# A fixed order for the projection steps of a perceiver layer, and low parts made one step earlier

## The chip, the core and the metric

The kernel runs on one core of a Trainium2 chip. The metric is the device time of one execution in microseconds. The core has five engines with a queue each, which run in order and wait for one another through semaphores: TensorE (PE, with its weight loads PEld), VectorE (DVE), ScalarE (ACT), GpSimd (POOL) and SyncE (SP), which issues nearly all DMAs here.

## What is computed

A perceiver layer over 128 latent rows of width 512. Its three blocks are a cross-attention of the normalised x over a context of 12544 rows, a chunked linear attention, and a quantised feed-forward part. Only the first block matters here:

```python
q = (inputs_q @ Wq).reshape(b, sq, H, HD) * (1.0 / np.sqrt(HD))
k = (inputs_kv @ Wk).reshape(b, skv, H, HD)
v = (inputs_kv @ Wv).reshape(b, skv, H, HD)
scores = jnp.einsum('bqhd,bkhd->bhqk', q, k)
attn = jax.nn.softmax(scores, axis=-1)
ctx = jnp.einsum('bhqk,bkhd->bqhd', attn, v).reshape(b, sq, H * HD)
return ctx @ Wo
```

with 16 heads of 128. The layer then goes on with `x = x + ...` for this block and the other two.

## The kernel before

**Projection stage.** q is projected and multiplied by Wk at once, so that the scores can be taken against the context itself. The loop over `h2` (eight pairs of heads) runs `project_q(h2 + 1)` ahead of `project_k(h2)`: PE makes `pq` (L205), ACT scales it into `qT` (L213), PE makes `pk` from `qT` and `wk` (L221), ACT copies `pk` into `b` in two halves (L230). In the text pq0 to pq7, qT0 to qT7, pk0 to pk7, b0 to b7 are these for each `h2`. Pairs 0 to 3 give the first half of the heads (f = 0), pairs 4 to 7 the second (f = 1); each half has two tiles `b` in a pool of three buffers.

**Strassen operands.** The products of the score stage are done in seven products instead of eight (Strassen-Winograd), each in three float32r products of high and low parts. `operands` makes the sums of the right side on DVE (L240: b11, t2, b12, b21), and `put` makes an operand's high part with an ACT cast (L233) and its low part with a DVE subtraction (L234). The names are B11, T2, T3, T1, T4, B21, B22. Half 0 is put during the projection loop, half 1 beside the first score units (the list `beside`). For the left side `sum_ct` makes four sums of a context block on DVE (L157 to L160) and `split_ct` its high part `cth` on ACT (L166) and its low part on DVE (L167).

**Score stage.** `scores` runs 49 blocks times 2 halves; a unit has 42 matmuls (L300). Its first product p1 needs A11 and B11, the second, p6, S2 and T2. p5 takes a second product only when DVE has read its first into c22 (L325). Results go to DRAM.

**Weighing stage.** 196 steps of 24 matmuls (L362): `soften(k)` subtracts the maximum on DVE (L410) and takes exp on ACT (L411), `high_part(k)` casts on ACT (L416) to `ph`, `low_part(k)` subtracts on DVE (L421) to `pl`, `total(k)` adds up on DVE (L429), `cut_hi` and `cut_lo` do the same split for the context rows (`ch` L398, `cl` L404). At a few steps `jobs` insert other work, among them an all-reduce of the sums on POOL (L554).

**Order.** A scheduler places instructions on the engines; those wrapped in `seq` keep their program order. Before, in the projection stage only the last sum of `sum_ct` is wrapped; in the weighing stage all steps are. `reuse` of a tile makes the next writer wait for the last reader. Weights are loaded into `ctp`'s tags "hi" and "lo", two buffers each, and pairs 2 and 3 into tiles of the right pool, `kq1p`. The DMA queue holds eight loads in flight.

Of the kernel before, what the change touches and what calls it, by code (L numbers as in the profile page):

```python
# [8 lines left out]
F32 = mybir.dt.float32  # L9
# [7 lines left out]
P = 128  # L17
# [3 lines left out]
HD = 128  # L21
# [12 lines left out]
def tile_perceiver_layer(  # L34
# [106 lines left out]
    def right(f, s, n):  # L141

        if (f, s) not in kq:
            kq[f, s] = (kq0p, kq1p)[f].tile([P, 2, 2, 512], F32R, name=f"kq{f}_{s}")
        return kq[f, s][:, n, :, :]

    def load_ct(i):
        if i == 1:
            raw = kq1p.tile([P, 8, 2, P], F32, name=f"kq1_{B22}")
        else:  # L150
            raw = ctp.tile([P, 8, 2, P], F32, tag="raw", name="ctr", bufs=1)
        nc.sync.dma_start(out=raw[:, A11:, :, :], in_=cT[i])
        return raw

    def sum_ct(raw):
        r = lambda s: raw[:, s, :, :]
        nc.vector.tensor_tensor(r(S1), r(A21), r(A22), ALU.add)  # L157
        nc.vector.tensor_tensor(r(S3), r(A11), r(A21), ALU.subtract)
        nc.vector.tensor_tensor(r(S2), r(S1), r(A11), ALU.subtract)
        seq(nc.vector.tensor_tensor(r(S4), r(A12), r(S2), ALU.subtract))  # L160

    def split_ct(raw, lo=None):
        hi = ctp.tile([P, 7, 2, P], F32R, tag="hi", name="cth")
        if lo is None:
            lo = ctp.tile([P, 7, 2, P], F32R, tag="lo", name="ctl")
        nc.scalar.copy(hi, raw[:, :7, :, :])  # L166
        nc.vector.tensor_tensor(lo, raw[:, :7, :, :], hi, ALU.subtract)  # L167
        return hi, lo


    with tc.tile_pool(name="ps_pro", bufs=2, space=PSUM) as ps_pro:

        def load_w(h2):

            hs = slice(h2 * 256, (h2 + 1) * 256)
            if h2 in (2, 3):
                both = kq1p.tile([P, 2, 1024], F32, name=f"kq1_{h2 + 2}")
                wq = both[:, 0, :].rearrange("p (c e) -> p c e", c=NC)
                wk = both[:, 1, :].rearrange("p (h d) -> p h d", h=2)
            else:  # L180
                wq = ctp.tile([P, NC, 256], F32, tag="hi", name="wq")
                wk = ctp.tile([P, 2, D], F32, tag="lo", name="wk")
            nc.sync.dma_start(out=wq, in_=x_wq[:, hs].rearrange("(c p) e -> p c e", p=P))
            nc.sync.dma_start(out=wk, in_=x_wkT[hs, :].rearrange("(h p) d -> p h d", p=P))
            return wq, wk

        keep_warm(ps_pro, 9)
        ws = [load_w(h2) for h2 in range(4)]
        raw = load_ct(0)
        xn = mxp.tile([P, D], F32, tag="mx1", name="xn")  # L190
        layernorm(xn, x0, D)

        warm = const.tile([P, 1], F32, name="warm")
        seq(nc.scalar.activation(warm, x0[:, 0:1], AF.Exp))
        xnT = tmp.tile([P, NC, P], F32, tag="u3", name="xnT")
        pt = ps_pro.tile([P, NC, P], F32, tag="q", name="pt")
        for i in range(NC):
            nc.tensor.transpose(pt[:, i, :], xn[:, i * P : (i + 1) * P], ident)
        nc.vector.tensor_copy(xnT, pt)

        def project_q(h2):
            pq = ps_pro.tile([P, 2, P], F32, tag="q", name="pq")
            for j in range(2):
                for cc in range(NC):
                    nc.tensor.matmul(  # L205
                        pq[:, j, :],
                        lhsT=ws[h2][0][:, cc, j * HD : (j + 1) * HD],
                        rhs=xnT[:, cc, :],
                        start=(cc == 0),
                        stop=(cc == NC - 1),  # L210
                    )
            qT = tmp.tile([P, 2, P], F32, tag=("p1", "u2")[h2 % 2], name="qT")
            nc.scalar.mul(qT, pq, HD**-0.5)  # L213
            return qT

        def project_k(h2, qT, b):

            pk = ps_pro.tile([P, 2, 2, 256], F32, tag="k", name="pk")
            for cc in range(NC):
                for j in range(2):  # L220
                    nc.tensor.matmul(  # L221
                        pk[:, cc // 2, cc % 2, j * P : (j + 1) * P],
                        lhsT=ws[h2][1][:, j, cc * P : (cc + 1) * P],
                        rhs=qT[:, j, :],
                        start=True,
                        stop=True,
                    )
            o = h2 % 2 * 256
            for a in range(2):
                nc.scalar.copy(b[h2 // 2 % 2][:, a, :, o : o + 256], pk[:, a, :, :])  # L230

        def put(f, s, v):
            nc.scalar.copy(right(f, s, 0), v)  # L233
            nc.vector.tensor_tensor(right(f, s, 1), v, right(f, s, 0), ALU.subtract)  # L234

        def operands(f, b):

            (b11, b21), (b12, b22) = ((t[:, 0, :, :], t[:, 1, :, :]) for t in b)
            t2 = mxp.tile([P, 2, 512], F32, tag=f"mx{f}", name="t2")
            sub = lambda out, x, y: nc.vector.tensor_tensor(out, x, y, ALU.subtract)  # L240
            return [
                lambda: sub(b11, b12, b11),
                lambda: sub(t2, b22, b11),
                lambda: put(f, T2, t2),
                lambda: sub(b12, b22, b12),
                lambda: put(f, T3, b12),
                lambda: put(f, T1, b11),
                lambda: sub(b21, b21, t2),
                lambda: put(f, T4, b21),
                lambda: put(f, B22, b22),  # L250
            ]

        qT = project_q(0)
        for h2 in range(8):
            if h2 + 4 < 8:
                ws.append(load_w(h2 + 4))
            if h2 == 1:
                raw1 = load_ct(1)
            nxt = project_q(h2 + 1) if h2 + 1 < 8 else None
            if h2 % 4 == 0:  # L260
                b = [iop.tile([P, 2, 2, 512], F32, tag="io", name="b") for _ in range(2)]
            project_k(h2, qT, b)
            qT = nxt
            if h2 == 1:
                put(0, B11, b[0][:, 0, :, :])
                put(0, B21, b[0][:, 1, :, :])
            if h2 == 2:
                sum_ct(raw)
            if h2 == 3:
                rest = operands(0, b)  # L270
                for do in rest[:6]:
                    do()
            if h2 == 5:
                cts = {0: split_ct(raw, mbp.tile([P, 7, 2, P], F32R, name="mb"))}
                for do in rest[6:]:
                    do()

    both = mbp.tile([P, 2, 1024], F32, name="mb")
    mb = [both[:, f, :] for f in range(2)]
# [2 lines left out]
    ps_s = psx.enter_context(tc.tile_pool(name="ps_s", bufs=8, space=PSUM, reuse_waits="tile"))  # L282
    beside = operands(1, b)
    beside[6:6] = [lambda: put(1, B21, b[0][:, 1, :, :])]
    beside[:0] = [
        lambda: (sum_ct(raw1), cts.update({1: split_ct(raw1)})), lambda: put(1, B11, b[0][:, 0, :, :]),
    ]

    def more():
        if beside:  # L290
# [61 lines left out]
    def weigh_operand(tag, n):  # L352
        return prp.tile([P, 1024], F32R, tag=tag, name=tag, bufs=n)
# [52 lines left out]
    def soften(k):  # L406
        f, i, j = step(k)
        if f is not None:
            exps[k] = scs[f, i][:, j, :]
            seq(nc.vector.tensor_tensor(exps[k], exps[k], mb[f], ALU.subtract))  # L410
            seq(nc.scalar.activation(exps[k], exps[k], AF.Exp))  # L411
# [5 lines left out]

    def low_part(k):
        if k < len(steps):
            low[k] = weigh_operand("pl", 2)  # L420
            seq(nc.vector.tensor_tensor(low[k], exps[k], high[k], ALU.subtract))  # L421

    def total(k):
        f, i, j = step(k)
        if f is not None:
            if i == 0 and j == 0:
                seq(nc.vector.tensor_copy(lsum[f], exps[k]))
            else:
                seq(nc.vector.tensor_tensor(lsum[f], lsum[f], exps[k], ALU.add))  # L429
# [5 lines left out]
    for i, f in units:  # L435
# [18 lines left out]
        while beside and (i, f) == (1, 0):  # L454
            more()
        if i + 1 not in cts and i + 1 < NP and i > 0 and (f == 1 or i == NP - 2):
            sum_ct(raw)
            cts[i + 1] = split_ct(raw)
        if (i, f) == (NP - 1, 0):
            nc.gpsimd.partition_all_reduce(mb[0], mx[0], P, bass_isa.ReduceOp.max)  # L460
    load_scores(2)
# [102 lines left out]
    at(4 * NP - 3, lambda: wo.update({1: by_rows(x_wo, 1, score_tile)}))  # L564

    with tc.tile_pool(name="ps_u", bufs=1, space=PSUM, reuse_waits="tile") as ps_u:
        total(0)
        soften(2)
        load_scores(4)
        for k, (f, i, j) in enumerate(steps):  # L570
            first, last = i == 0 and j == 0, i == NP - 1 and j == 1
# [13 lines left out]
                            seq(nc.scalar.copy(dst, old[b][cc]))  # L585
            high_part(k + 2)
            cut_hi(k + 2)
            low_part(k + 1)
            soften(k + 3)
            cut_lo(k + 1)  # L590
            total(k + 1)
            if k == 2:
                last_max()
            load_scores(k + 5)
            load_ctx(k + 3)
            weigh(pu, j, ctx_hi[f, i], ctx_lo[f, i], high.pop(k), low.pop(k), first, last)
            old = pu
            for job, args in jobs.pop(k, ()):
# [351 lines left out]
```

## Time and profile before

| | us |
|---|---|
| median of 3 runs | 2140.52 (2140.45 to 2141.22) |
| the profiled execution, its time | 2139.74 |
| its span | 2138.0 |
| projection stage, start to first score product | 0 to 37.3 |
| score stage | 37.3 to 972.7 |
| weighing stage | 972.7 to 2041 |
| rest of the layer | 2041 to 2138 |

The stages are read off the timeline of PE. In the table of groups a score or weighing matmul of 512 columns has a duration of 389 ns, but they are pipelined and follow each other every 0.227 us, so that a unit takes 9.52 us and a weighing step 5.44. In timeline lines the first two numbers are start and duration; in brackets stands how long the engine had been idle and which instruction ended that. In lists of waits the numbers are the total, how often, and the longest.

### The profile page before, as it was taken

The page shows a single profiled execution, that of the slowest core. Times are in us where ns is not written, and L with a number is a line of the kernel's source. Part 1 is how long each engine was busy: PE and PEld are TensorE (multiplying, and loading weights), DVE is VectorE, ACT ScalarE, POOL GpSimd, SP SyncE. Part 2 cuts the span into 40 slices and gives each one's busy share as a digit, 9 for nine tenths or more (in the row PEclk, how much of TensorE's full clock was granted, in tenths as well). Part 3 has the DMA queues.
Part 4 walks back from the last instruction along what each step waited for, and adds up shares of the span by engine and source line. Part 5 has one row for each costly group of instructions (what it writes and reads, how often), then busy time and mean ns, then how long its engine had stood idle before and what let it go on. Part 6 is the DMA issues. An engine that isn't in the chain of part 4 may idle for free.

```text
span 2138.0 us, 24043 instructions
## 1 busy us (share of the span) xinstructions
PE 2123.8 (99%) x9561; PEld 1739.7 (81%) x9566; DVE 1657.6 (78%) x1812; ACT 763.9 (36%) x843; POOL 24.8 (1%) x16
## 2 busy tenths in 40 slices
PE   9999999999999999999999999999999999999998
PEld 7888888888888888888888888888888888888874
DVE  6877777777777777778997888887887777777735
ACT  5222122221222212215444444444444444444423
POOL 0000000000000000000000000000100000000010
PEclk9999999999999999999999999999999999999999
DMA  6444444444444444446664455554444444444460
GB/s 221 149 172 160 169 177 157 167 162 163 177 160 165 167 158 177 165 150 226 222 231 151 170 173 186 187 187 148 138 148 148 141 140 144 147 148 148 139 205 9
DMA packets 77393, 350.36 MB, mean 164 GB/s; under 512 B 8000, under 2 KB 12352, under 8 KB 51808
## 3 DMA queue, kind: packets, MB, share of 16 engines
q1 hardware_dynamic: 77136, 348.69, 45.8%
q8 instruction: 75, 1.23, 0.2%
q14 instruction: 38, 0.31, 0.0%
q10 hardware_dynamic: 144, 0.13, 0.0%
HBM read 245.77 MB, written 103.02 MB: 163 GB/s over the span
## 4 chain that ended last, share of the span: by engine, by line
PE 96%; DVE 2%; issue 1%; DMA 0%; ACT 0%; DVEq 0%; SPq 0%
PE pu L362 49%; PE ps L300 43%; PE pc L629 1%; PE po L648 1%; DMA kq<-in_cT_dram 0%; PE pp L722 0%; DVE kq L234 0%; PE pq L205 0%; PE pw L92 0%; DVE b L240 0%; PE ph L848 0%; PE pp L782 0%; PE po L766 0%; PE psc L761 0%; PE pk L221 0%
## 5 line engine op out<-in xcount | busy, mean ns | idle before, releaser
L300 PE MATMUL ps<-kq,cth 128*128 128x512 f32 x2744 | 844.6, 389 | 0.0
L362 PE MATMUL pu<-ph,cl 128*128 128x512 f32 x1568 | 610.2, 389 | 1.4 <-DVE cl L404 1.2
L362 PE MATMUL pu<-pl,ch 128*128 128x512 f32 x1568 | 610.0, 389 | 0.0
L362 PE MATMUL pu<-ph,ch 128*128 128x512 f32 x1568 | 610.0, 389 | 0.0
L300 PEld LDWEIGHTS ps<-kq,cth 128*128 128x128 f32 x2744 | 515.0, 188 | 106.8
L300 PE MATMUL ps<-kq,ctl 128*128 128x512 f32 x1344 | 522.8, 389 | 0.0
L421 DVE TENSOR_TENSOR pl<-si,ph 128x1024 fp32r<-128x1024 f32 x194 | 241.3, 1244 | 203.5 <-PE pu L362 201.8
L362 PEld LDWEIGHTS pu<-ph,cl 128*128 128x128 f32 x1568 | 294.3, 188 | 63.2 <-DVE cl L404 2.2
L362 PEld LDWEIGHTS pu<-pl,ch 128*128 128x128 f32 x1568 | 294.3, 188 | 61.3
L362 PEld LDWEIGHTS pu<-ph,ch 128*128 128x128 f32 x1568 | 294.3, 188 | 61.1
L416 ACT CAST ph<-si 128x1024 fp32r<-128x1024 f32 x194 | 204.0, 1052 | 389.9 <-PE pu L362 389.8
L300 PEld LDWEIGHTS ps<-kq,ctl 128*128 128x128 f32 x1344 | 252.3, 188 | 52.5
L334 ACT COPY so<-ps 128x512 f32<-128x512 f32 x98 | 57.8, 589 | 577.0 <-PE ps L300 577.0
L411 ACT ACTIVATE si<-si 128x1024 f32<-128x1024 f32 x194 | 205.3, 1058 | 116.6 <-DVE si L410 116.4
L410 DVE TENSOR_TENSOR si<-si,mb 128x1024 f32<-128x1024 f32 x194 | 236.6, 1219 | 0.0
L429 DVE TENSOR_TENSOR lsum<-lsum,si 128x1024 f32<-128x1024 f32 x192 | 234.0, 1219 | 0.0
L343 DVE TENSOR_TENSOR mx<-mx,so 128x1024 f32<-128x1024 f32 x95 | 116.4, 1225 | 9.6
L338 DVE TENSOR_TENSOR so<-ps,u 128x512 f32<-128x512 f32 x98 | 67.7, 691 | 72.2 <-PE ps L300 72.2
L404 DVE TENSOR_TENSOR cl<-cr,ch 128x1024 fp32r<-128x1024 f32 x98 | 119.5, 1219 | 0.5 <-ACT ch L398 0.5
L332 DVE TENSOR_TENSOR mx<-mx,so 128x1024 f32<-128x1024 f32 x95 | 116.5, 1227 | 3.2
L398 ACT CAST ch<-cr 128x1024 fp32r<-128x1024 f32 x98 | 103.3, 1054 | 40.5 <-DMA cr<-in_c_dram 40.3
L328 DVE TENSOR_TENSOR so<-ps,u 128x512 f32<-128x512 f32 x98 | 67.7, 691 | 61.3 <-PE ps L300 61.3
(190 smaller groups left out, 1005.8 us busy)
## 6 DMA issues: line engine op xcount, KB each, us to landing
sc<-so SPq DMA_DIRECT2D x98, 1024.0 KB, 3.8
si<-sc SPq DMA_DIRECT2D x97, 1024.0 KB, 4.8
cr<-in_c_dram SPq DMA_DIRECT2D x98, 512.0 KB, 3.4
ctr<-in_cT_dram SPq DMA_DIRECT2D x94, 512.0 KB, 3.5
kq<-in_w1T_dram SPq DMA_DIRECT2D x16, 512.0 KB, 4.9
kq<-in_w2T_dram SPq DMA_DIRECT2D x16, 512.0 KB, 4.9
wq<-in_x_wq_dram SPq DMA_DIRECT2D x6, 512.0 KB, 5.2
wk<-in_x_wkT_dram SPq DMA_DIRECT2D x6, 512.0 KB, 6.1
```

The lines of the kernel that those rows point to most:

```text
L300: nc.tensor.matmul(ps, lhsT=lt[:, a, cc, :], rhs=right(f, b, part)[:, cc, :], start=(first and n == 0), stop=(n == 5), skip_group_check=True,)
L328: nc.vector.tensor_tensor(c21, p4, u3, ALU.add)
L332: nc.vector.tensor_tensor(mx[f], mx[f], so[:, 1, :], ALU.max)
L343: nc.vector.tensor_tensor(mx[f], so[:, 1, :] if i == 0 else mx[f], so[:, 0, :], ALU.max)
L362: nc.tensor.matmul(pu[b][cc], lhsT=lt[:, j, cs], rhs=rt[:, bs], start=(first and n == 0), stop=(last and n == 2))
L398: seq(nc.scalar.copy(ctx_hi[f, i], ctx_raw[f, i]))
L404: seq(nc.vector.tensor_tensor(ctx_lo[f, i], ctx_raw[f, i], ctx_hi[f, i], ALU.subtract))
L410: seq(nc.vector.tensor_tensor(exps[k], exps[k], mb[f], ALU.subtract))
L411: seq(nc.scalar.activation(exps[k], exps[k], AF.Exp))
L416: seq(nc.scalar.copy(high[k], exps[k]))
L421: seq(nc.vector.tensor_tensor(low[k], exps[k], high[k], ALU.subtract))
L429: seq(nc.vector.tensor_tensor(lsum[f], lsum[f], exps[k], ALU.add))
```

## The change

It does three things. In the projection stage, what `put`, `operands`, `sum_ct`, `split_ct`, `project_q` and `project_k` issue for half 0 and for context blocks 0 and 1 is wrapped in `seq`; the sums and splits get other places in the loop (block 0 at h2 = 2, T2 at 3, T3 and T1 at 4, T4 and B22 at 5, block 1 at 6 instead of beside the first score units). Weights of pairs 2 to 7 go into right-operand tiles of half 1 that are free until then, and all loads are issued ahead of the loop. `xnT` is copied in two halves by two engines. In the weighing stage `low_part` and `cut_lo` are made for step k + 2 instead of k + 1, `pl` gets a third buffer, and `load_ctx` goes from k + 3 to k + 4.

```diff
+    def spare(s, shape):
+        return kq1p.tile(shape, F32, name=f"kq1_{s}")
+    def in_turn(i, instruction):
+        return seq(instruction) if i < 2 else instruction
...
-    def sum_ct(raw):
+    def sum_ct(raw, i):
         r = lambda s: raw[:, s, :, :]
-        nc.vector.tensor_tensor(r(S1), r(A21), r(A22), ALU.add)
+        in_turn(i, nc.vector.tensor_tensor(r(S1), r(A21), r(A22), ALU.add))
...
-        nc.scalar.copy(hi, raw[:, :7, :, :])
-        nc.vector.tensor_tensor(lo, raw[:, :7, :, :], hi, ALU.subtract)
+        in_turn(i, nc.scalar.copy(hi, raw[:, :7, :, :]))
+        in_turn(i, nc.vector.tensor_tensor(lo, raw[:, :7, :, :], hi, ALU.subtract))
...
-            if h2 in (2, 3):
-                both = kq1p.tile([P, 2, 1024], F32, name=f"kq1_{h2 + 2}")
+            if h2 >= 2:
+                both = spare((B11, B21, T2, T3, T1, T4)[h2 - 2], [P, 2, 1024])
...
-        ws = [load_w(h2) for h2 in range(4)]
-        raw = load_ct(0)
+        ws, raws = [], {}
+        for what in (0, 1, 2, 3, "ct0", 4, 5, "ct1", 6, 7):
...
-        nc.vector.tensor_copy(xnT, pt)
+        nc.vector.tensor_copy(xnT[:, :2, :], pt[:, :2, :])
+        nc.scalar.copy(xnT[:, 2:, :], pt[:, 2:, :])
...
-            nc.scalar.mul(qT, pq, HD**-0.5)
+            seq(nc.scalar.mul(qT, pq, HD**-0.5))
...
-                nc.scalar.copy(b[h2 // 2 % 2][:, a, :, o : o + 256], pk[:, a, :, :])
+                seq(nc.scalar.copy(b[h2 // 2 % 2][:, a, :, o : o + 256], pk[:, a, :, :]))
...
-            nc.scalar.copy(right(f, s, 0), v)
-            nc.vector.tensor_tensor(right(f, s, 1), v, right(f, s, 0), ALU.subtract)
+            in_turn(2 * f, nc.scalar.copy(right(f, s, 0), v))
+            in_turn(2 * f, nc.vector.tensor_tensor(right(f, s, 1), v, right(f, s, 0), ALU.subtract))
...
             if h2 == 2:
-                sum_ct(raw)
+                sum_ct(raws[0], 0)
+                cts = {0: split_ct(raws[0], 0, mbp.tile([P, 7, 2, P], F32R, name="mb"))}
             if h2 == 3:
                 rest = operands(0, b)
-                for do in rest[:6]:
-                    do()
-            if h2 == 5:
-                cts = {0: split_ct(raw, mbp.tile([P, 7, 2, P], F32R, name="mb"))}
-                for do in rest[6:]:
-                    do()
+            for do in rest[slice(*{3: (0, 3), 4: (3, 6), 5: (6, 9)}.get(h2, (0, 0)))] if h2 >= 3 else ():
+                do()
+            if h2 == 6:
+                sum_ct(raws[1], 1)
+                cts[1] = split_ct(raws[1], 1)
...
-            low[k] = weigh_operand("pl", 2)
+            low[k] = weigh_operand("pl", 3)
...
+        low_part(1)
+        soften(2)
         total(0)
-        soften(2)
...
-            low_part(k + 1)
             soften(k + 3)
-            cut_lo(k + 1)
+            cut_lo(k + 2)
+            low_part(k + 2)
             total(k + 1)
...
-            load_ctx(k + 3)
+            load_ctx(k + 4)
```

More of the change, by code (lines that the diff above doesn't have):

```diff
@@ L145, in right @@
         return kq[f, s][:, n, :, :]
+    def spare(s, shape):
+        return kq1p.tile(shape, F32, name=f"kq1_{s}")
+    def in_turn(i, instruction):
+        return seq(instruction) if i < 2 else instruction
     def load_ct(i):
         if i == 1:
-            raw = kq1p.tile([P, 8, 2, P], F32, name=f"kq1_{B22}")
+            raw = spare(B22, [P, 8, 2, P])
         else:
@@ L153, in load_ct, with split_ct @@
         return raw
-    def sum_ct(raw):
+    def sum_ct(raw, i):
         r = lambda s: raw[:, s, :, :]
-        nc.vector.tensor_tensor(r(S1), r(A21), r(A22), ALU.add)
-        nc.vector.tensor_tensor(r(S3), r(A11), r(A21), ALU.subtract)
-        nc.vector.tensor_tensor(r(S2), r(S1), r(A11), ALU.subtract)
+        in_turn(i, nc.vector.tensor_tensor(r(S1), r(A21), r(A22), ALU.add))
+        in_turn(i, nc.vector.tensor_tensor(r(S3), r(A11), r(A21), ALU.subtract))
+        in_turn(i, nc.vector.tensor_tensor(r(S2), r(S1), r(A11), ALU.subtract))
         seq(nc.vector.tensor_tensor(r(S4), r(A12), r(S2), ALU.subtract))
-    def split_ct(raw, lo=None):
+    def split_ct(raw, i, lo=None):
         hi = ctp.tile([P, 7, 2, P], F32R, tag="hi", name="cth")
@@ L187, in tile_perceiver_layer @@
         keep_warm(ps_pro, 9)
-        ws = [load_w(h2) for h2 in range(4)]
-        raw = load_ct(0)
+        ws, raws = [], {}
+        for what in (0, 1, 2, 3, "ct0", 4, 5, "ct1", 6, 7):
+            if what == "ct0":
+                raws[0] = load_ct(0)
+            elif what == "ct1":
+                raws[1] = load_ct(1)
+            else:
+                ws.append(load_w(what))
         xn = mxp.tile([P, D], F32, tag="mx1", name="xn")
@@ L239, in operands @@
             t2 = mxp.tile([P, 2, 512], F32, tag=f"mx{f}", name="t2")
-            sub = lambda out, x, y: nc.vector.tensor_tensor(out, x, y, ALU.subtract)
+            sub = lambda out, x, y: in_turn(2 * f, nc.vector.tensor_tensor(out, x, y, ALU.subtract))
             return [
@@ L254, in tile_perceiver_layer @@
         for h2 in range(8):
[L255 to L258, printed above, removed]
             nxt = project_q(h2 + 1) if h2 + 1 < 8 else None
@@ L284, in tile_perceiver_layer @@
     beside[6:6] = [lambda: put(1, B21, b[0][:, 1, :, :])]
-    beside[:0] = [
-        lambda: (sum_ct(raw1), cts.update({1: split_ct(raw1)})), lambda: put(1, B11, b[0][:, 0, :, :]),
-    ]
+    beside[:0] = [lambda: put(1, B11, b[0][:, 0, :, :])]
     def more():
@@ L456, in tile_perceiver_layer @@
         if i + 1 not in cts and i + 1 < NP and i > 0 and (f == 1 or i == NP - 2):
-            sum_ct(raw)
-            cts[i + 1] = split_ct(raw)
+            sum_ct(raw, i + 1)
+            cts[i + 1] = split_ct(raw, i + 1)
         if (i, f) == (NP - 1, 0):
```

## The prediction

> **What bounds it now.** I read the page's shares and chain first, then the waits of TensorE (PE), then the timelines of ScalarE (ACT) and VectorE (DVE) around each wait.
>
> ```profile
> span 2138.0 us, 24043 instructions
> PE 2123.8 (99%) x9561; PEld 1739.7 (81%) x9566; DVE 1657.6 (78%) x1812; ACT 763.9 (36%) x843; POOL 24.8 (1%) x16
> ...
> PE 96%; DVE 2%; issue 1%; DMA 0%; ACT 0%; DVEq 0%; SPq 0%
> ```
>
> PE is the bound: nothing the change does shortens its 96% of the chain, so the time can move only by PE's waits. These are all the waits of PE before the closing stage that a step of the change can touch:
>
> ```profile
> PE pu L362 <- DVE cl L404: 1.2, 1, 1.2
> ...
> PE ps L300 <- ACT b L230: 1.0, 1, 1.0
> PE pk L221 <- ACT qT L213: 1.0, 1, 1.0
> PE pq L205 <- DVE xnT L199: 0.8, 1, 0.8
> PE ps L300 <- DVE so L325: 0.7, 1, 0.7
> ```
>
> Three facts follow. No wait of PE names a weight's DMA, so loading the weights earlier removes no wait. In the projection stage PE waits 0.96 + 1.02 + 0.66 = 2.64 us for ACT and DVE (the times that the timeline gives at 35.49, 39.96 and 47.72 us). In 196 weighing steps it waits once, at 1551 us, and hardly (0.32 us) at 983.54. So the change can win at most some 4.7 us (2.64, 0.32 and 1.2 with their slow restarts, 0.27 at xnT); what it can lose is whatever its fixed order makes ACT and DVE late.
>
> The rows that I cost with (start, duration, engine, line, tiles):
>
> ```profile
> 16.70 1.07 ACT L230 COPY b<-pk 128x512 f32<-128x512 f32 x2 [1.34 <-PE pk L221]
> 17.66 2.00 ACT L233 CAST kq<-b 128x1024 fp32r<-128x1024 f32 x2
> ...
> 27.89 0.38 ACT L213 ACTIVATE qT<-pq 128x256 f32<-128x256 f32 x1
> ...
> 31.54 1.69 ACT L166 CAST cth<-ctr 128x1792 fp32r<-128x1792 f32 x1
> ```
> ```profile
> 25.69 1.22 DVE L240 TENSOR_TENSOR b<-b 128x1024 f32<-128x1024 f32 x1
> ...
> 33.97 2.02 DVE L167 TENSOR_TENSOR mb<-ctr,cth 128x1792 fp32r<-128x1792 f32 x1
> 35.91 2.35 DVE L234 TENSOR_TENSOR kq<-b,kq 128x1024 fp32r<-128x1024 f32 x2
> ```
>
> Followers on one engine start sooner than the duration says: a cast every 0.96 us, a 1024-wide DVE step every 1.14 us (two in 2.35), a low part of a context block every 1.94, a pair of b copies 0.97. A group of 16 PE records takes 1.79.
>
> **Projection stage, the main term.** The diff pins nearly every ACT and DVE step in program order. Read off the built order, ACT now runs: qT3, b2, cth of block 0, qT4, b3, cast T2, qT5, b4, casts T3 and T1, qT6, b5, casts B11 and B21 of the second half (they are not pinned and land here), casts T4 and B22, qT7, b6, cth of block 1, b7. Before, a qT was squeezed in ahead of casts that waited; now qT5 to qT7, which PE's pk5 to pk7 need, stand behind casts that themselves wait for DVE. I walk the three queues from before's 7.2 us with the rows above (the same walk over before's order puts PE's three restarts at 34.7, 39.2 and 47.0, within 0.8 us of the trace).
>
> DVE: low parts of B11 and B21 at 18.42, the sums of block 0 (four, 0.34 each and one wait of 0.11) 20.69 to 22.24. Before, those sums ran at 16.98, in a hole; now they stand behind the two low parts. ACT's cth 22.26 to 23.95; DVE's low part of the block 23.98 to 26.00 (before, it came only after the steps that follow here, at 33.97); b11 25.92, t2 needs its result, 27.17 to 28.39. So ACT, through with b3 at 25.2, waits 3.3 us for t2 and casts T2 at 28.42; qT5 29.38 to 29.76; PE was free for pk5 at 28.69 and starts at 29.80: **1.11 us**. DVE's T2 low part 29.50, b12 30.63 to 31.85; ACT casts T3 31.89, T1 32.84, qT6 33.80 to 34.18; pk6 starts at 34.22 instead of 33.48: **0.74**. ACT then has no hole: b5 34.09, the two casts of the second half 35.08 and 36.04, T4 37.00, B22 37.95, qT7 38.91 to 39.29; pk7 starts at 39.33, PE was free at 36.11: **3.22**. b6 must wait for T4's low part to free its tile (39.90): 39.94 to 41.0. The sums of block 1 stand on DVE behind B22's low part (39.82) and have a sum of block 2 among them: 40.95 to 42.74. cth of block 1 waits for them, 42.77 to 44.46, and b7 behind it ends at 45.42. b7 frees the PSUM bank of the second score product, which could have started at 42.57: 45.46, **2.89**. DVE goes on with the low part of block 1 44.48, b11, the B22 low part, t2, b12 of the second half (46.42 to 51.1), and only then u2 51.03, a low part, u3 52.79, a low part, c22 54.54 to 55.23; p5's second product must wait for c22: 55.27 instead of 52.36, **2.91**.
>
> Sum of waits 10.87 against 2.64: +8.23. The halves of xnT: DVE's would end at 7.15 (0.43, the row of a 128x256 copy at L710) instead of 7.42, but ACT's half waits for DVE's and ends 0.38 later, 7.55, in time for the third matmul only; I take -0.2, bounds -0.27 and +0.1. The weight loads cost nothing: before's loads land 1.4 us apart (by issue and time to landing: 4.95, 7.2, 8.6 and so on to 24.6 for block 1), and their order is nearly kept, so the last four land at about 26.0 (wq6), 27.4, 28.8 (wq7) and 30.2; PE needs wq6 at 26.9 and wq7 at 31.6. The cover is 0.9 us; without it a late wq6 costs its lateness, less the 1.11 us that pk5 waits anyway. The walk was up to 0.8 us early over before, and five waits follow each other here, whose errors are partly the same one: bounds of -3 to +2 on the stage.
>
> **Weighing stage, what goes.** At the all-reduce of lsum the timeline has
>
> ```profile
> 1544.37 4.44 DVE L421 TENSOR_TENSOR pl<-si,ph 128x1024 fp32r<-128x1024 f32 x1 [1.34 <-PE pu L362]
> ...
> 1551.14 0.50 PE L362 MATMUL pu<-ph,cl 128*128 128x512 f32 x1 [1.21 <-DVE cl L404]
> ```
>
> POOL's PARTITION_ALL_REDUCE runs from 1543.20 for 6.12 us; the DVE step beside it takes 4.44 instead of 1.22, and cl, due in the next step, is 1.2 us late. With cl and pl made two steps (10.88 us) ahead a delay of 3.2 us is covered: -1.21, and -0.14 for the ten slow matmuls after the restart (0.24 instead of 0.227, the first 0.34). In the new order the step beside the reduction is a subtraction that waits for no PE; even if it ended with the reduction, at 1549.3, its followers end before 1556 and are due at 1560.
>
> [...]
>
> **Weighing stage, what comes.** At the start the steps stand closer. Before, DVE filled its wait for the cast of step 1 with total(0) and the subtraction of step 2; now low_part(1) stands ahead of them and DVE waits 2.3 us for exp and cast (1.06 + 1.05). Counted from the first weighing matmul (972.66 before): pl(1) ends at +5.4 as before, in time; the subtraction of step 2 runs +5.3 to +6.6 instead of +2.5; exp, cast and ch on ACT to +9.7; cl(2) ends +10.9 and pl(2) +12.05, due at +10.88 and +11.1. PE loses 0.09 + 0.91 and 0.1 of slow restart, where it lost 0.42: +0.7 (bounds 0 and +1.2). Steps 3 to 6 are in time again by 1.5 us or more. Steady state: DVE has 7 steps of 1.14 and two jobs of up to 1.14 in 10.88 us, 10.3 at most, with a step more of slack: 0. SP's order: load_ctx is issued a step earlier behind cl; it lands in 3.4 us and no PE waits on it. The third pl buffer adds no copy.
>
> **Sum.** +8.23 - 0.2 + 0.7 - 1.35 = +7.4 us: span 2145.4, and 1.74 around it as now (2139.74 - 2138.0) gives 2147.1. The median shown is 0.8 above the profiled run: 2147.9; forecast **2147.7**.
>
> The granted clock is 1.0 in every slice to the last, and no wait of PE here is over 1.3 us. [...]
>
> **Rivals.** (1) The fixed order runs through, as the change says: no wait in the projection stage, none at the start of weighing: -2.64 - 0.27 - 0.42 - 1.35 = -4.7, 2135.8: faster. Place: ACT's queue between b3 and qT5; it decides if t2 is ready when b3 ends, near 25.2. For: ACT is busy for 30 of the first 48 us, so there is room. Against: t2 comes three DVE steps after cth, at 28.4 by rows alone. 4%. (2) PE's new waits are half as long, because sums or block low parts run sooner than I walk: +4.1 + 0.7 - 1.35 - 0.2 = +3.2, 2143.8. For: the walk was up to 0.8 us early on before. Against: DVE is without a hole from 33 to 43 us in it. 13%. (3) The projection stage comes out even, only the weighing terms count: -0.65, 2139.9. 6%. (4) More than I sum, by a late wq6 and the upper bounds of both stages (+2 and +0.5): 2150.4 and above. 6%. Forecast: 71%.
>
> **Numbers.** Within 0.2% (4.3 us, about what a measurement can tell here) of 2140.5 means up to 2144.8. Slower by more: 71 + 6 + 6 (the upper half of rival 2) = 83%; same: 7 + 6 = 13%; faster 4%. The range reaches into rival 2: 2143.5 to 2150.5.
>
> **What would show it.** Five waits of PE before 60 us: three on qT (pk5 to pk7, the last the longest), one on b at the second score product, one on so (c22); ACT's longest waits at the T2 cast, DVE's on cth. In the weighing stage none at 1551 us, and one of about a microsecond on pl in the third step. I am wrong if pk7 starts without a wait, or if the first score products follow pk7 unbroken.

## The result and the profile after

| | before | changed |
|---|---|---|
| median, us | 2140.51 (2140.45 to 2141.22, 6 runs) | 2148.38 (2147.0 to 2150.44, 6 runs) |
| the profiled execution, its time / its span | 2139.74 / 2138.0 | 2148.01 / 2146.3 |
| PE starts pk0 | 11.14 | 12.08 |
| from there to the first weighing matmul | 961.52 | 969.55 |
| from there to the end of the span | 1165.34 | 1164.67 |

The ratio of the runs is 1.0037 [1.0024, 1.005]: slower by 7.9 us, or 0.37%. The three lower rows are read off PE's timeline and split the 8.3 us by which the span grew: +0.94 at the start, +8.03 in the projection stage and the first score products, -0.67 in the weighing stage and behind it.

The page's shares of the changed kernel:

```profile
span 2146.3 us, 23938 instructions
PE 2123.8 (99%) x9561; PEld 1740.0 (81%) x9566; DVE 1652.9 (77%) x1812; ACT 754.7 (35%) x844; POOL 27.4 (1%) x16
```

PE is busy for the same 2123.8 us as before; DVE and ACT are busy a little less. The time is all in waits of PE. Its list of waits (total, how often, the longest), in the changed kernel's line numbers (pk L236, second and later score products L309, weighing L371):

```profile
PE pk L236 <- ACT qT L228: 4.7, 3, 3.0
PE ps L309 <- ACT b L245: 2.7, 1, 2.7
PE ps L309 <- DVE so L334: 2.7, 1, 2.7
...
PE pq L220 <- DMA wq<-in_x_wq_dram: 1.3, 1, 1.3
...
PE pu L371 <- DVE pl L430: 0.7, 1, 0.7
```

The five waits that were walked are there: three for qT, one for b7 (the second score product), one for c22 (the `so` of L334). The wait for cl at the all-reduce is gone; the one for pl in the third weighing step has come. A wait for the DMA of pair 1's wq was not foreseen.

Which of these set the end is not in that list but in the chain of waits. These are pieces of it in order of time (start, duration, engine, tile, line):

```profile
23.55 1.69 ACT cth L174
25.27 2.03 DVE mb L175
27.29 1.15 DVE b L255
28.54 1.24 DVE t L255
29.80 1.05 ACT kq L248
...
37.82 4.62 DVE kq L249 x4
44.15 1.69 ACT cth L174
45.87 2.04 DVE ctl L175
...
51.34 1.22 DVE b L255
56.68 925.13 PE ps L309 x4080
```

From 17.64 to 56.68 us the chain does not touch PE once. It goes back and forth between ACT and DVE: block 0's cast, its low part, b11, t2, the cast of T2; later block 1's cast and low part; at last c22. PE's waits for qT at 31, 35 and 40 us lie beside this chain, not on it.

In the weighing stage the lines that answer to those shown of before are (PE, then DVE and POOL):

```profile
993.90 0.47 PE L371 MATMUL pu<-pl,ch 128*128 128x512 f32 x1 [0.73 <-DVE pl L430]
```
```profile
1556.08 5.56 DVE L430 TENSOR_TENSOR pl<-si,ph 128x1024 fp32r<-128x1024 f32 x1
```
```profile
1555.19 6.95 POOL L563 PARTITION_ALL_REDUCE mb<-lsum  x1 [93.86 <-DVE lsum L562]
```

A DVE step is again stretched beside the reduction, this time to 5.56 us, and PE does not wait: the low parts are two steps ahead.

### The profile page after: what moved, and what is told of

Read it like the earlier page. It is cut to its first block, busy times and chain, and to the rows that moved or that the text cites. A ratio compares the mean times of both kernels' runs of the same rounds, so it can differ in the third digit from the quotient of the medians.

```text
span 2146.3 us, 23938 instructions
## 1 busy us (share of the span) xinstructions
PE 2123.8 (99%) x9561; PEld 1740.0 (81%) x9566; DVE 1652.9 (77%) x1812; ACT 754.7 (35%) x844; POOL 27.4 (1%) x16
## 4 chain that ended last, share of the span: by engine, by line
PE 96%; DVE 2%; ACT 1%; issue 0%; DMA 0%; SPq 0%; DVEq 0%; ACTq 0%
PE pu L371 49%; PE ps L309 43%; PE pc L639 1%; PE po L658 1%; DVE kq L249 0%; DMA wq<-in_x_wq_dram 0%; PE pp L732 0%; PE pw L92 0%; DVE b L255 0%; ACT kq L248 0%; PE pq L220 0%; PE ph L858 0%; PE pp L792 0%; PE po L776 0%; PE psc L771 0%
## 5 line engine op out<-in xcount | busy, mean ns | idle before, releaser
L309 PE MATMUL ps<-kq,cth 128*128 128x512 f32 x2744 | 844.9, 389 | 0.0
L371 PE MATMUL pu<-pl,ch 128*128 128x512 f32 x1568 | 610.0, 389 | 0.7 <-DVE pl L430 0.7
L371 PE MATMUL pu<-ph,cl 128*128 128x512 f32 x1568 | 610.1, 389 | 0.0
L371 PE MATMUL pu<-ph,ch 128*128 128x512 f32 x1568 | 610.0, 389 | 0.0
L309 PEld LDWEIGHTS ps<-kq,cth 128*128 128x128 f32 x2744 | 515.2, 188 | 106.8
L309 PE MATMUL ps<-kq,ctl 128*128 128x512 f32 x1344 | 522.8, 389 | 0.0
L371 PEld LDWEIGHTS pu<-pl,ch 128*128 128x128 f32 x1568 | 294.3, 188 | 62.3 <-ACT ph L425 1.0
L371 PEld LDWEIGHTS pu<-ph,cl 128*128 128x128 f32 x1568 | 294.3, 188 | 61.4 <-DVE cl L413 0.4
L371 PEld LDWEIGHTS pu<-ph,ch 128*128 128x128 f32 x1568 | 294.3, 188 | 61.0
L309 PEld LDWEIGHTS ps<-kq,ctl 128*128 128x128 f32 x1344 | 252.3, 188 | 52.2
```

Source lines behind the costliest of these rows:

```text
L309: nc.tensor.matmul(ps, lhsT=lt[:, a, cc, :], rhs=right(f, b, part)[:, cc, :], start=(first and n == 0), stop=(n == 5), skip_group_check=True,)
L371: nc.tensor.matmul(pu[b][cc], lhsT=lt[:, j, cs], rhs=rt[:, bs], start=(first and n == 0), stop=(last and n == 2))
```

## The experiments

Each kernel was timed beside the kernel before on its chip (medians there 2140.6 to 2140.7). Ratios are to that.

**The weighing part alone**, put on the kernel before:

```diff
-            low_part(k + 1)
             soften(k + 3)
-            cut_lo(k + 1)
+            cut_lo(k + 2)
+            low_part(k + 2)
...
-        total(0)
-        soften(2)
+        low_part(1)
+        soften(2)
+        total(0)
```
(and the third buffer of pl and load_ctx at k + 4)

> The kernel before with the weighing part of the change alone (cl and pl two steps ahead, third pl buffer, load_ctx at k + 4, low_part(1) ahead of soften(2) and total(0)). By the sum of the prediction: -1.35 for the wait at the all-reduce, +0.7 for the third step: 2139.9, between 2139.3 and 2140.6; PE's wait on cl near 1551 us is gone, one of 0.6 to 0.9 us on pl stands in the third step. Rival, the weighing part costs as much as it wins or more (VectorE loses time in every step): 2140.5 or above.

Measured: 2140.09, ratio 0.9996 [0.9987, 1.0005]. The wait for cl is gone from the list, one of 0.73 for pl has come. The size fits; by time alone it can't be told from no change.

**The weights in free operands alone**, all loads ahead of the loop, nothing pinned that was not pinned before:

```diff
-            if h2 in (2, 3):
+            if h2 >= 2:
...
+        ws += [load_w(h2) for h2 in (4, 5)]
+        raw1 = load_ct(1)
+        ws += [load_w(h2) for h2 in (6, 7)]
...
-            if h2 + 4 < 8:
-                ws.append(load_w(h2 + 4))
```

> The kernel before with the weights of pairs 2 to 7 in free right operands and all loads issued ahead of the loop, nothing pinned, xnT in one piece, weighing as before. My theory: no wait of PE was on a weight, so there is little to win; block 1 comes earlier, and PE waits for b at the second score product and for c22 some 0.8 us each: 2139.7, between 2139 and 2140.6. Rival, the early loads delay the first ones and the wait of 1.33 us on wq1 in the changed kernel's trace belongs to them: 2141 to 2142, runs spread by 1 us or more, and PE waits over 0.5 us for wq at the second group.

Measured: 2139.38, ratio 0.9996 [0.9987, 1.0004]: no loss that the times can show; the rival's 2141 to 2142 falls. PE waits 0.32 us for b and 0.60 for c22, and not at all for a weight's DMA. That last point tells little here: in this profile pq0 and pq1 themselves were slow (6.62 us instead of 3.68), so that pq1 came late by itself.

**The projection part alone**: the changed kernel with the weighing part undone.

> The changed kernel with its weighing part undone: the projection part alone. My theory: all of the loss is here, so 2148.4 + 0.65 = 2149.0, between 2148 and 2150.5; PE's five waits before 60 us as in the changed kernel (1.1, 0.6, 3.0 on qT, 2.7 on b, 2.7 on so), and the wait on cl at the all-reduce is back with 1.2 us. Rival, part of the loss is in the weighing stage: 2146 to 2147.5.

Measured: 2150.03, ratio 1.0042 [1.003, 1.0055], a microsecond more than expected. The profiled execution was the fastest of the five (2149.03), but its stage from pk0 to the first weighing matmul is 1.6 us longer than in the changed kernel. PE's timeline shows where that went:

```profile
55.78 0.50 PE L309 MATMUL ps<-kq,mb 128*128 128x512 f32 x1 [2.74 <-DVE so L334]
...
56.98 1.05 PE L309 MATMUL ps<-kq,cth 128*128 128x512 f32 x2
57.84 0.63 PE L309 MATMUL ps<-kq,ctl 128*128 128x512 f32 x1
```

After the wait for c22 a pair of matmuls takes 1.05 us instead of 0.62: PE's granted clock is 0.61 from 55.78 to 59.5 us. No wait comes behind this one, so the 1.6 us that it costs stay in the sum. Whether the slower executions lose at the same place is not shown.

**Nothing pinned**: the changed kernel with the new wrappers of the projection stage taken off; places in the loop, weights and weighing part as in the changed kernel.

```diff
-        return seq(instruction) if i < 2 else instruction
+        return instruction
...
-            seq(nc.scalar.mul(qT, pq, HD**-0.5))
+            nc.scalar.mul(qT, pq, HD**-0.5)
...
-                seq(nc.scalar.copy(b[h2 // 2 % 2][:, a, :, o : o + 256], pk[:, a, :, :]))
+                nc.scalar.copy(b[h2 // 2 % 2][:, a, :, o : o + 256], pk[:, a, :, :])
```

> The changed kernel with nothing of the projection stage kept in program order but the last sum of a block, as before; weights in free operands, the new places in the program and the weighing part stay. My theory, the fixed order is the loss: 2139.9 if wq1 is in time, up to 2141.5 if it is late; PE waits for qT 0.3 at most, for b 1.4, for so 1.2. Rival, the new places of the steps or the weight loads are the loss: 2146 or above, with the waits of the changed kernel.

Measured: 2139.6, ratio 0.9994 [0.9985, 1.0003]. The whole loss comes with the pins: with the scheduler free, the weights and the new places in the program cost nothing that can be measured. PE waits 1.5 us for qT (0.3 at most was expected), 1.0 for b and 0.9 for c22.

**Which steps of the order?** Two kernels, one edit each. Block 1 late:

```diff
-            if h2 == 6:
+            if h2 == 7:
                 sum_ct(raws[1], 1)
                 cts[1] = split_ct(raws[1], 1)
```

> The changed kernel with one number altered: the sums and the split of context block 1 are issued at h2 = 7, behind b7, instead of at h2 = 6, ahead of it; everything stays pinned. Theory (the end of the projection stage is set by what ACT and DVE hand each other: b7 stands on ACT behind the cast of block 1, which waits for four sums on DVE): b7 no longer waits, so the 2.74 us of PE at the second score product goes, and the wait for c22 (2.73) falls to about 1.0, since DVE's steps of the second half come sooner; the three waits for qT (4.7 us) stay as they are. Walked by the rows: 4.9 us less than the changed kernel, about 2143.5. Rival (DVE has the same steps to do in any order, so that the wait taken away comes back at c22): about 2148.4, with a c22 wait near 5.5.

Measured: 2143.68, ratio 1.0013 [1.0004, 1.0022]: 4.7 less than the changed kernel. The list of waits has the three for qT unchanged (4.7), none for b7, and 0.7 for c22. The rival, that the wait comes back at c22, falls. One thing was not expected; PE's timeline:

```profile
41.19 3.68 PE L236 MATMUL pk<-qT,kq 128*128 128x128 f32 x16 [2.98 <-ACT qT L228]
...
56.55 0.50 PE L309 MATMUL ps<-kq,mb 128*128 128x512 f32 x1 [0.71 <-DVE so L334]
```

In this execution pk7 ran at half the clock after its wait (0.51 granted from 41.19 to 44.5 us): 3.39 us from its start to the next group's (44.58) instead of 1.81 in the changed kernel (40.68 to 42.49). That made b7 and with it DVE's steps of the second half 1.57 us late. It was the slowest of the 11 runs (2145.21); the 4.9 walked holds for the median.

Only qT free:

```diff
-            seq(nc.scalar.mul(qT, pq, HD**-0.5))
+            nc.scalar.mul(qT, pq, HD**-0.5)
```

> The changed kernel with one wrapper taken off: the scaling of pq into qT is free again to be placed where the scheduler likes; all the other steps stay pinned. Theory (PE's waits for qT are a symptom: the end of the stage is set by the chain through DVE's sums and the casts, which does not get shorter): the three qT waits (4.7 us) vanish, and PE waits at the second score product for as much longer as it comes there earlier, about 8 us instead of 2.74, with the c22 wait as before near 2.8; the time stays at 2148.4, within 0.5. Rival (the qT waits themselves are the loss, each adding to the end): 2143.7, with the second score product's wait near 2.7 as before.

Measured: 2147.32, ratio 1.0031 [1.0019, 1.0042]; the interval holds the changed kernel's ratio and lies above the rival's 2143.7 (1.0014). PE's timeline:

```profile
47.28 0.80 PE L309 MATMUL ps<-kq,mb 128*128 128x512 f32 x1 [7.78 <-ACT b L245]
...
57.09 0.50 PE L309 MATMUL ps<-kq,mb 128*128 128x512 f32 x1 [0.76 <-DVE so L334]
```

All but 0.18 of the 4.7 us for qT are gone, and PE waits 7.78 instead of 2.74 for b7. From pk0's start to the first weighing matmul it takes 969.55 us, as the changed kernel does to the hundredth. The c22 wait is shorter (0.76, expected near 2.8), for a reason of its own: after 7.78 us of idling PE's clock is 0.51 from 47.28 to 51.5 us, the matmuls lose 1.9 us there, and the wait behind them is shorter by as much. The median is 1.1 below the changed kernel's, more than the 0.5 allowed for; what makes it so is not shown.

**Another order, still pinned.** What is left with block 1 late, some 4 us against nothing pinned, stands in DVE's waits between 25 and 35 us of the changed kernel: 1.75 for block 0's cast, 1.11 for the cast of T2, 1.17 for that of T3. So all steps were left pinned and DVE's order changed:

```diff
             if h2 == 1:
+                sum_ct(raws[0], 0)
                 put(0, B11, b[0][:, 0, :, :])
...
             if h2 == 2:
-                sum_ct(raws[0], 0)
-                cts = {0: split_ct(raws[0], 0, mbp.tile([P, 7, 2, P], F32R, name="mb"))}
+                hi = high_ct(raws[0], 0)
             if h2 == 3:
                 rest = operands(0, b)
+                rest[2:4] = rest[3:1:-1]
...
+            if h2 == 3:
+                cts = {0: low_ct(raws[0], 0, hi, mbp.tile([P, 7, 2, P], F32R, name="mb"))}
-            if h2 == 6:
+            if h2 == 7:
                 sum_ct(raws[1], 1)
```
(`high_ct` and `low_ct` are the two halves of `split_ct`; at h2 = 3 four entries of `rest` are made, at 4 two)

> The changed kernel, all steps still pinned, but in another order: block 1 at h2 = 7 (as in the run above that did only this), the sums of block 0 ahead of the low parts of B11 and B21, b12 ahead of the low part of T2, and the low part of block 0 behind T2's. Theory (what the changed kernel loses is the order in which ACT and DVE hand each other work, not that the order is fixed): DVE no longer waits for the cast of block 0 (1.75 us) nor for the cast of T2 (1.11), pk5 and pk6 start without a wait, pk7 still waits about 2.9; by the rows c22 comes 1.85 us sooner than with block 1 late alone, and PE has two matmuls more to do ahead of it: 2.3 us less than that run's 2143.7, about 2141.4. Rival (a fixed order costs this by itself, wherever the steps stand): 2143.7, with the waits of DVE only moved.

Measured: 2140.5, ratio 0.9999 [0.999, 1.0008]: 3.2 less than with block 1 late alone, 7.9 less than the changed kernel, with every step pinned that the change pins. DVE's timeline:

```profile
24.25 1.22 DVE L264 TENSOR_TENSOR b<-b 128x1024 f32<-128x1024 f32 x1 [3.14 <-ACT b L254]
...
27.92 1.23 DVE L258 TENSOR_TENSOR kq<-t,kq 128x1024 fp32r<-128x1024 f32 x1
29.06 2.02 DVE L176 TENSOR_TENSOR mb<-ctr,cth 128x1792 fp32r<-128x1792 f32 x1
```

T2's low part and block 0's now start without a wait (no bracket behind them), and from 24.25 us DVE runs without a listed wait to 60. PE waits 2.05 at pk7 (about 2.9 was expected) and 0.59 at c22, together what it waited before the change. The rival, that a fixed order costs by itself, falls. Which of the moves beside block 1's brings the 3.2 was not tried one by one.

**The old order at the start of weighing**, on the changed kernel:

```diff
-        low_part(1)
-        soften(2)
-        total(0)
+        total(0)
+        soften(2)
+        low_part(1)
```

> The changed kernel with the old order at the start of the weighing stage: total(0), soften(2), then low_part(1). Theory (the wait for pl in the third weighing step comes from low_part(1) standing ahead of the subtraction of step 2): the wait of 0.73 us and the slow restart of 0.3 go: 2147.4. Rival (the wait comes from low parts being made a step ahead at all, whatever the order at the start): a wait of 0.7 or more in the third step stays, 2148.4 or above.

Measured: 2147.71, ratio 1.0032 [1.002, 1.0044]. The time can't be told from the changed kernel's. The trace can: the wait for pl is gone from the list, and the part from the first weighing matmul on takes 1163.42 us against 1164.67.

**What beats both.** The kernel before with the parts that did not lose, and no new pin in the projection stage: free operands, low parts a step further ahead, the old start.

> The kernel before with the parts that did not lose, and no fixed order in the projection stage: weights of pairs 2 to 7 in free right operands with all loads ahead, low parts of the weighing made a step further ahead, and the old order at its start. Theory (only the fixed order loses; the other parts gain what their waits were): the wait at the all-reduce (1.35) and that at the start of weighing (0.3) go, and 0.5 to 0.8 in the projection stage: 2138.0 to 2138.5, against 2140.5 before. Rival (the projection stage's gain is given back at the first score products, and the start of weighing loses as in the changed kernel): 2139.6 to 2140.1.

Measured: 2138.15 (2137.06 to 2139.06, 11 runs), ratio 0.9986 [0.9977, 0.9995]: faster than before by 0.14%. To see what the operands add, the same without them:

> The kernel before with the low parts of the weighing stage a step further ahead and the old order at its start; weights and loads as before. Theory (the gain of the combined version over before is that of the weighing stage, whose part of the profile is 1.9 us shorter there): 2138.7, within 0.2% of the combined version's 2138.15. Rival (weights in free operands with all loads ahead give a part of it): 2139.5 or more.

Measured: 2139.08, ratio 0.9992 [0.9983, 1.0], between the two expectations. Its interval overlaps that of the combined version; whether the free operands give any part of the gain stays open. In the combined version's profile the gain lies in the weighing stage alone: the first weighing matmul starts at 973.01 us, before the change at 972.66. The 0.5 to 0.8 expected in the projection stage is not there.

All profiles side by side, in us: PE's start of pk0, from there to the first weighing matmul, and from there to the end.

| | median | pk0 | to weighing | rest |
|---|---|---|---|---|
| before | 2140.5 | 11.14 | 961.52 | 1165.34 |
| changed | 2148.4 | 12.08 | 969.55 | 1164.67 |
| weighing part alone | 2140.1 | 12.31 | 961.31 | 1164.98 |
| projection part alone | 2150.0 | 11.17 | 971.16 | 1164.97 |
| free operands alone | 2139.4 | 14.43 | 959.54 | 1165.03 |
| nothing pinned | 2139.6 | 11.59 | 962.83 | 1164.68 |
| block 1 late | 2143.7 | 12.60 | 966.20 | 1164.70 |
| qT free | 2147.3 | 12.49 | 969.55 | 1164.66 |
| reordered | 2140.5 | 10.93 | 961.80 | 1164.67 |
| old start | 2147.7 | 11.15 | 969.53 | 1163.42 |
| weighing with the old start | 2139.1 | 11.88 | 962.78 | 1163.74 |
| combined | 2138.15 | 11.01 | 962.00 | 1163.39 |

The third column tells the losing order (966 to 971) from the others (960 to 963). The last tells the weighing: 1164.97 to 1165.34 as before, 1164.66 to 1164.98 a step further ahead with the new start, 1163.39 to 1163.74 with the old one. The first varies by more than a microsecond among kernels with the same start; its 14.43 comes from pq0 and pq1, which took 6.62 us there (7.81 to 14.43) instead of 3.68 before (5.14 with block 1 late, 5.16 with qT free). At 3.31 a group that is about the pace of pk7 at half the clock (3.39). That PE ran at half the clock in these groups is an estimate from the two paces; no profile shows it, and PE's clock is listed as 1.00 from 0 to 14 us in all three.

The last column can be split where PE starts its first matmul behind the weighing stage (2040.92 us before, 2049.12 changed). The weighing stage alone takes 1068.21 to 1068.26 us in the three kernels with the weighing of before, 1067.49 to 1067.52 in the six with the new start and 1066.24 to 1066.26 in the three with the old one. The part behind it takes 96.76 to 97.50, in no such order, and makes up most of the spread of the last column within each of the three.

## Why the prediction was right

The forecast was 2147.7 in 2143.5 to 2150.5 (the sum itself gave 2147.9); the median is 2148.38. Sum against sum, it was +7.4 for the profiled execution and the time grew by 8.27.

| step of the prediction | predicted | measured |
|---|---|---|
| pk5 behind the cast of T2 | 1.11 | 1.07 |
| pk6 behind that of T3 | 0.74 | 0.63 |
| pk7 behind the casts of B11, B21, T4, B22 | 3.22 | 2.98 |
| second score product, b7 behind block 1's cast | 2.89 | 2.74 |
| p5's second product, c22 at the end of DVE's queue | 2.91 | 2.73 |
| sum, against 2.64 before | 10.87 | 10.15 |
| start of the stage (halves of xnT) | -0.2 | +0.94 |
| weighing stage, net | -0.65 | -0.77 |
| part behind it | 0 | +0.10 |

*Projection stage.* The queues walked by rows were right in place, cause and order, each wait 0.04 to 0.24 too long. From pk0 on the stage grew by 8.03 for the 8.23 of the sum: 7.51 in waits, the rest in slower matmuls behind each restart (pk5's group took 1.89 us, 31.18 to 33.07, instead of 1.79), a term that the sum did not have. Waits 0.72 too long and a missing term of 0.52 nearly cancel; that the sum came so close is partly luck, the places and the order are not.

*The reading of the five waits* is where more was learned than forecast. The sum treats them as five terms. The runs show that they are one chain seen from PE: with qT freed 4.7 us of them vanish and the stage takes as long; with block 1 moved by one turn of the loop 4.7 us vanish from the time, though the qT waits stay. Their sum was right since all five were walked along the same queues; as prices of single edits they would have been wrong.

*Start.* The halves of xnT do start pq0 sooner (6.83 for 7.46; DVE's half ends at 6.78, ACT's follows in time), 0.27 of it by the shorter wait. The mis-sized term is the cost of the loads at nothing: pq1 waited 1.33 us for wq1. The cover that was named was for wq6; wq1 was not looked at. But it is not the change's: the weighing part alone, whose loads are those of before, shows a wait of 1.01 at the same place, and the projection part alone, with the changed loads, one of 0.23. pk0's start varies from 10.93 to 14.43 in the table, and by over a microsecond among kernels with one and the same order of loads (11.15 to 12.60).

*Weighing.* The all-reduce wait went, and the third step lost 0.73 and its restart, as walked. The stage takes 1067.49 us instead of 1068.26. The -0.67 of the first table also holds the part behind the stage, which was 0.10 longer in this profile. Both sides of the net were a little small: the new start loses 1.25 against the old one (1.1 was walked: 0.09, 0.91 and 0.1 of slow restart), and all else gains 2.0 (1.77 was walked: 1.35 at the all-reduce and the 0.42 that the start of before lost). The two misses nearly cancel in the net.

*Clock.* The sum has no term for a lower clock. In the profile shown none was needed (1.00 granted behind all three waits of 2.7 to 3 us); in other kernels' profiles the clock is 0.51 to 0.61 behind four such waits (below). That profile is not typical: the mean granted clock over the whole execution was 1.000 in it and 0.997 to 0.999 in the other five executions of the changed kernel, while it was 1.000 in 54 of the 71 executions of the kernel before that were timed beside the experiments. That the median, unlike the profile, holds some lower clock is an estimate from these means.

*Rivals.* A fixed order that runs through (2135.8) did not come: b3 ended at 26.49, t2 at 29.77, 3.3 us after it, as walked; the reordered kernel shows that it needed another order and not less pinning, and even it comes to 2140.5 only. Half waits, an even stage and more than the sum fall by the table.

## What to carry to other kernels

A wait at the engine that bounds the kernel tells where it stood, not what made it late: free the thing waited for, and if the end does not move, the chain lies elsewhere. Before pinning steps of two engines that feed each other, write both queues side by side with durations and look for a step that waits for the other engine while work that is ready stands behind it; here block 1's sums ahead of b7 were 4.7 us of the loss, and the order of DVE's steps for block 0, T2 and b12 the other 3.2. Pinning itself cost nothing that could be measured once the order had no such place, and gained nothing over the scheduler's own.

## What the runs showed of the hardware

**The clock after a wait of about 3 us went either way.** Of eight waits of PE of 2.7 to 3.0 us in these profiles (three in the changed kernel, two each in the projection part alone and in the changed kernel with the old start, one with block 1 late) four were followed by about half the clock and four by 1.00; the one of 7.78 us was followed by half the clock too. The granted clock in these stretches:

| kernel | wait before it, us | stretch, us | granted clock |
|---|---|---|---|
| projection part alone | 2.98 | 39.77 to 43.0 | 0.51 |
| projection part alone | 2.74 | 55.78 to 59.5 | 0.61 |
| block 1 late | 2.98 | 41.19 to 44.5 | 0.51 |
| old start | 2.74 | 45.93 to 48.9 | 0.52 |
| qT free | 7.78 | 47.28 to 51.5 | 0.51 |

The same wait of 2.98 us for qT7 left 1.00 in the changed kernel (40.6 to 42.4 us) and 0.51 with block 1 late. Each time the lower clock cost 1.3 to 1.9 us of PE, but it lengthened the run only where no wait came behind it (1.6 us in the projection part alone), or where DVE waited for the slowed matmuls (1.57 us with block 1 late). What decides which way it goes is not shown.

**DVE beside the all-reduce.** The subtraction that takes 1.22 us alone took 4.44 beside the reduction in the kernel before and in the projection part alone, and 5.56 in the changed kernel, the weighing part alone and the combined version; the reduction took 6.12 in the first two and 6.94 or 6.95 in the other three. The subtraction ahead of it in the changed kernel, from 1554.94, ran for a microsecond beside the reduction (from 1555.19) in its usual 1.22 us. What stretches the one and not the other is not shown; spans on POOL are rough.

**Loads in flight.** By their times of issue and landing at most seven loads were in flight in the kernel before, and eight in the changed kernel, at each of the nine issues from 9.77 to 20.26 us.
